# Routing tokens to pages of 128 rows per expert in a four-layer block (attention, experts, RWKV, experts)

## The chip, the cores and the metric

The kernel runs on one core of one Trainium2 chip. The metric is the device time of one execution in microseconds (us); all data are float32 in device memory before and after.

## The reference

`x` has 8 sequences of 512 tokens and 128 channels. It passes four layers, each `x = x + layer(layernorm(x))`: causal attention, a mixture of experts, an RWKV block (with layernorms of its own), and the same mixture of experts again. Cut to the experts, which the change is about:

```python
scores = softmax(xf @ Wg)                       # xf: 4096 tokens x 128, 32 experts
weights, indices = top_k(scores, 4)
C = 4 * (4096 * 4) // 32                        # 2048: tokens that one expert takes at most
for e in range(32):
    pos = nonzero(pair_expert == e, size=C)     # the first C (token, expert) pairs in token order
    xg = xf[tok]
    out = (silu(xg @ W1[e]) * (xg @ W3[e])) @ W2[e] * w[:, None]     # 64 hidden units
    y = y.at[tok].add(out)
z = (silu(xf @ Ws1) * (xf @ Ws3)) @ Ws2         # the shared expert, 128 hidden units
return y + z
```

The RWKV block runs a recurrence over the tokens, which the kernel does with scans along the free axis on VectorE, and a channel mix with a hidden width of 512 whose hidden values are `relu(.)**2`.

## The kernel before

A sequence is held as four tiles of 128 tokens (`NJ`). Each layer is a generator that issues a few instructions per step.

- `attention(b)` (from L277): layernorm, four transposes (`turn`, L153), Q, K, V, then four blocks of scores, softmax, transposes and products, and then `route(x, 0, b)`.
- `rwkv(b)` (from L351): two layernorms one behind the other (`norm`, L137, each with an addition and a power on POOL, L146 and L147), projections, three scans, four reciprocals, the output projection, the channel mix, then `route(x, 1, b)`. Ten of its elementwise operations on 128x512 are on POOL, and the four squares of L449.
- `route(xa, f, b)` (L160): layernorm, the scores `lg`, the four largest (`chosen`, L194), running counts per expert (L201 on POOL, L205 and L206 on PE), and gates: the score where an expert was chosen and has room, else zero. The gates are transposed and stored to `gd` in memory (L216).
- `experts(f, b)` (L230): all 32 experts on all 512 tokens. Two experts fill 128 partitions, so 16 pairs, plus the shared expert as step 0. A pair has two matmuls into PSUM, `a` (L251) and `c` (L253), tanh on ACT (L257), a DVE operation (L258), a multiplication by the gates on DVE (L263), a product on POOL (L264), and a matmul that accumulates into `y` (L239). Where the gate is zero, the work is done and contributes nothing. The gates of four pairs are read back from `gd`, each over 64 partitions, by two loads on SP's queue (L224): eight loads per call.

The sequences go through the layers one behind the other: in step `s` of the loop at L477, `experts(0, s-1)` is interleaved with `attention(s)`, and `experts(1, s-3)` with `rwkv(s-2)`, one step of the experts to two of the other. A scheduler then orders the instructions of each engine by dependences and priorities, so the order is near the written one and not equal to it. Engines work in order and wait for one another by semaphores.

Of the kernel before, what the change touches and what calls it, by code (L numbers as in the profile page):

```python
# [9 lines left out]
F32 = mybir.dt.float32  # L10
AF = mybir.ActivationFunctionType
ALU = mybir.AluOpType
AX = mybir.AxisListType
PSUM = bass.MemoryType.PSUM

P = 128          # partitions, tokens of a tile, channels
B = 8            # sequences
S = 512          # tokens of a sequence
NJ = S // P      # token tiles of a sequence
E = 32           # experts  # L20
NP = E // 2      # expert pairs: two experts of 64 hidden units fill 128 partitions
NQ = NP // 4     # gate loads of a sequence, each for four pairs
TOPK = 4
CAP = 4 * (B * S * TOPK) // E   # tokens that one expert takes at most
# [3 lines left out]
# Columns of the packed [128, .] weights.  # L28
# [9 lines left out]
# Columns of the packed per-channel vectors.  # L38
# [4 lines left out]
def interleave(heavy, light):  # L43
    """Traces two streams of work side by side: two steps of the light one behind each of the heavy one."""
    for _ in heavy:
        for _ in range(2):
            next(light, None)
    for _ in light:
        pass
# [3 lines left out]
def kernel(ctx: ExitStack, tc: tile.TileContext, x, small, vecs, w13, w2, out):  # L53
# [3 lines left out]
    xin = ctx.enter_context(tc.tile_pool(name="xin", bufs=3))  # L57
    wk2 = ctx.enter_context(tc.tile_pool(name="wk2", bufs=2))
    wk1 = ctx.enter_context(tc.tile_pool(name="wk1", bufs=1))
    mo = ctx.enter_context(tc.tile_pool(name="mo", bufs=3))  # L60
    gates = ctx.enter_context(tc.tile_pool(name="gates", bufs=2))
    st = ctx.enter_context(tc.tile_pool(name="st", bufs=3))
    dram = ctx.enter_context(tc.tile_pool(name="dram", bufs=2, space=bass.MemoryType.DRAM))
    ps_m = ctx.enter_context(tc.tile_pool(name="ps_m", bufs=2, space=PSUM))
    ps_y = ctx.enter_context(tc.tile_pool(name="ps_y", bufs=1, space=PSUM))
    ps_l = ctx.enter_context(tc.tile_pool(name="ps_l", bufs=3, space=PSUM))

# [15 lines left out]
    w13s = const.tile([P, NP, 2, P], F32, tag="w13", name="w13s")  # L83
    w2s = const.tile([P, NP, P], F32, tag="w2", name="w2s")
    for q in range(NQ):
        nc.sync.dma_start(out=w13s[:, 4 * q : 4 * q + 4], in_=w13[:, 4 * q : 4 * q + 4])
        nc.sync.dma_start(out=w2s[:, 4 * q : 4 * q + 4], in_=w2[:, 4 * q : 4 * q + 4])
    load_x(1)

# [15 lines left out]
    tri = const.tile([P, P], F32, tag="tri", name="tri")     # tri[i, t] = i <= t  # L105
# [3 lines left out]
    nhalf = const.tile([P, NJ], F32, tag="nhalf", name="nhalf")  # L109
    nc.gpsimd.memset(nhalf, -0.5)  # L110
    wdec = const.tile([P, 1], F32, tag="wdec", name="wdec")  # -exp(time_decay)
    nc.scalar.activation(wdec, V("time_decay"), AF.Exp)
    nc.vector.tensor_scalar(wdec, wdec, -1.0, None, ALU.mult)

    # Scores and the values looked for in them, each behind or before four marks that every row
    # has: the match below then finds just the four largest, the first of equals first.
    sc, lst, tot = [], [], []
    for f in range(2):
        s = const.tile([P, NJ, E + 4], F32, tag=f"sc{f}", name=f"sc{f}")
        m = const.tile([P, NJ, 8], F32, tag=f"lst{f}", name=f"lst{f}")  # L120
        for i in range(4):
            nc.gpsimd.memset(s[:, :, E + i : E + i + 1], -1.0 - i)
            nc.gpsimd.memset(m[:, :, 4 + i : 5 + i], -1.0 - i)
        t = wk2.tile([P, NJ + 1, E], F32, tag=f"tot{f}", name=f"tot{f}_start")
        nc.gpsimd.memset(t[:, NJ, :], 0.0)
        sc.append(s)
        lst.append(m)
        tot.append(t)
# [8 lines left out]
    def norm(src, dst, name):  # L137
        """dst = (src - mean) / sqrt(var + eps) over the channels of [128 tokens, 4, 128]."""
        stats = st.tile([P, NJ, 6], F32, tag="stats", name=f"stats_{name}")
        mv = st.tile([P, NJ, 2], F32, tag="mv", name=f"mv_{name}")  # L140
        rstd = st.tile([P, NJ], F32, tag="rstd", name=f"rstd_{name}")
        for j in range(NJ):
            nc.vector.bn_stats(out=stats[:, j, :], in_=src[:, j, :])
        for j in range(NJ):
            nc.vector.bn_aggr(out=mv[:, j, :], in_=stats[:, j, :])  # L145
        nc.gpsimd.tensor_scalar(rstd, mv[:, :, 1], EPS, None, ALU.add)  # L146
        nc.gpsimd.tensor_tensor(rstd, rstd, nhalf, ALU.pow)  # L147
# [5 lines left out]
    def turn(src, name):  # L153
        """[128 tokens, 4, 128 channels] -> PSUM [128 channels, 512 tokens], or back."""
        p = light(f"turn_{name}")
        for j in range(NJ):
            nc.tensor.transpose(p[:, j * P : (j + 1) * P], src[:, j * P : (j + 1) * P], ident)  # L157
        return p

    def route(xa, f, b):  # L160
        """Layernorm, scores, the top four experts, capacity; gates go out over the partitions of
        their experts. Gates carry the factor 1/2 of silu(a) = a (1 + tanh(a/2)) / 2."""
        n = f"{f}_{b}"
        xn = wk1.tile([P, NJ, P], F32, tag=f"xn{f}", name=f"xn_{n}")
# [3 lines left out]
        xT = wk2.tile([P, S], F32, tag=f"fT{f}", name=f"fT_{n}")  # L168
# [7 lines left out]
        ex = wk1.tile([P, NJ, E], F32, tag=f"ex{f}", name=f"ex_{n}")  # L176
# [13 lines left out]
        rep = wk1.tile([P, NJ, E + 4], F32, tag=f"rep{f}", name=f"rep_{n}")  # L190
        for j in range(NJ):
            nc.vector.match_replace(out=rep[:, j, :], in_to_replace=m[:, j, :], in_values=s[:, j, :], imm_value=-9.0)
        chosen = wk1.tile([P, NJ, E], F32, tag=f"chosen{f}", name=f"chosen_{n}")
        nc.vector.tensor_scalar(chosen, rep[:, :, :E], -5.0, None, ALU.is_lt)  # L194
        gate = wk1.tile([P, NJ, E], F32, tag=f"gate{f}", name=f"gate_{n}")
        nc.vector.scalar_tensor_tensor(gate, s[:, :, :E], 0.5, chosen, ALU.mult, ALU.mult)
        # tot[j] counts, per place in a tile, the tokens of earlier tiles that chose an expert.
        t = wk2.tile([P, NJ + 1, E], F32, tag=f"tot{f}", name=f"tot_{n}")
        nc.gpsimd.tensor_copy(t[:, 0, :], tot[f][:, NJ, :])
        for j in range(NJ):  # L200
            nc.gpsimd.tensor_tensor(t[:, j + 1, :], t[:, j, :], chosen[:, j, :], ALU.add)  # L201
        tot[f] = t
        yield
        cum = light(f"cum_{n}")[:, : NJ * E]
        nc.tensor.matmul(cum, tri, flat(chosen), start=True, stop=False)  # L205
        nc.tensor.matmul(cum, ones, flat(t[:, :NJ, :]), start=False, stop=True)  # L206
        wt = wk1.tile([P, NJ * E], F32, tag=f"wt{f}", name=f"wt_{n}")
        nc.vector.scalar_tensor_tensor(wt, cum, float(CAP), flat(gate), ALU.is_le, ALU.mult)
        yield
        p = light(f"wT_{n}")  # L210
        for j in range(NJ):
            nc.tensor.transpose(p[:E, j * P : (j + 1) * P], wt[:, j * E : (j + 1) * E], ident)
        wT = wk1.tile([E, S], F32, tag=f"wT{f}", name=f"wT_{n}")
        nc.scalar.copy(wT, p[:E, :])
        gd = dram.tile([E, S], F32, tag=f"gd{f}", name=f"gd_{n}")
        nc.sync.dma_start(out=gd, in_=wT)  # L216
        yield
        gv = gd.rearrange("(q i two) t -> two q i t", two=2, q=NQ)

        def load_gates(q):  # L220
            """The gates of four pairs, each over the 64 partitions of its expert."""
# [307 lines left out]
```

## Time and profile before

| | |
|---|---|
| time, median of 3 runs | 1131.81 us (1131.66 to 1132.06) |
| profiled execution | 1130.8 us span |
| PE (TensorE matmul) busy | 988.6 us, 87%, 2800 instructions |
| DVE (VectorE) busy | 746.7 us, 66%, 1809 instructions |
| POOL (GpSimd) busy | 565.0 us, 50%, 613 instructions |
| ACT (ScalarE) busy | 311.6 us, 28%, 578 instructions |
| DMA | 77.38 MB, 68 GB/s mean over the span |

The profile comes from one execution, recorded by the hardware. PEld is TensorE's weight load, which overlaps PE. A line of a group has the program line, the engine, the operation, output and inputs with their shapes, the count, then busy us and the mean in ns of one, and last the idle time of the engine just before the group with what ended most of it. PEclk is the clock that TensorE was granted, 1 being full speed. A float32 matmul runs as two passes and counts as two.

### The profile page before, as it was taken

The page shows a single profiled execution, that of the slowest core. Times are in us where ns is not written, and L with a number is a line of the kernel's source. Part 1 is how long each engine was busy: PE and PEld are TensorE (multiplying, and loading weights), DVE is VectorE, ACT ScalarE, POOL GpSimd, SP SyncE. Part 2 cuts the span into 40 slices and gives each one's busy share as a digit, 9 for nine tenths or more (in the row PEclk, how much of TensorE's full clock was granted, in tenths as well). Part 3 has the DMA queues.
Part 4 walks back from the last instruction along what each step waited for, and adds up shares of the span by engine and source line. Part 5 has one row for each costly group of instructions (what it writes and reads, how often), then busy time and mean ns, then how long its engine had stood idle before and what let it go on. Part 6 is the DMA issues. An engine that isn't in the chain of part 4 may idle for free.

```text
span 1130.8 us, 9602 instructions
## 1 busy us (share of the span) xinstructions
PE 988.6 (87%) x2800; PEld 457.6 (40%) x2800; DVE 746.7 (66%) x1809; ACT 311.6 (28%) x578; POOL 565.0 (50%) x613
## 2 busy tenths in 40 slices
PE   4798988799789987998889988899889998888988
PEld 2443543344334433454334543344334443333433
DVE  2456577766866767667776678567685649588543
ACT  2231323223323332232322323232222223231221
POOL 1134345643663457534674347544484547548433
PEclk8799999999999999999999999999999999999999
DMA  5053325105332241133313240331402340142051
GB/s 184 13 118 73 81 50 112 37 13 111 78 73 50 65 96 38 45 79 80 71 38 98 59 101 17 75 86 38 114 26 50 86 112 0 38 96 65 1 123 46
DMA packets 45668, 77.38 MB, mean 68 GB/s; under 512 B 2864, under 2 KB 11184, under 8 KB 45488
## 3 DMA queue, kind: packets, MB, share of 16 engines
q1 hardware_dynamic: 45472, 76.77, 29.1%
q8 instruction: 22, 0.36, 0.1%
q14 instruction: 30, 0.25, 0.1%
q10 hardware_dynamic: 144, 0.01, 0.0%
HBM read 73.62 MB, written 3.15 MB: 68 GB/s over the span
## 4 chain that ended last, share of the span: by engine, by line
PE 47%; DVE 30%; POOL 15%; issue 4%; DMA 2%; ACT 2%; SPq 0%; POOLq 0%; DVEq 0%; ACTq 0%
PE y L239 11%; PE a L251 10%; PE c L253 10%; DVE v L263 5%; POOL h L264 4%; DVE h L258 4%; PE kk L446 3%; PE kv L459 2%; DVE wden L416 2%; PE o L325 2%; PE s L307 2%; DVE xn L149 1%; POOL rstd_f L147 1%; POOL tot L201 1%; DVE sc L184 1%
## 5 line engine op out<-in xcount | busy, mean ns | idle before, releaser
L264 POOL TENSOR_TENSOR h<-h,v 128x512 f32<-128x512 f32 x256 | 336.7, 1316 | 374.4 <-DVE v L263 299.8
L257 ACT ACTIVATE h<-a 128x512 f32<-128x512 f32 x272 | 161.5, 596 | 497.2 <-PE a L251 462.1
L251 PE MATMUL a<-fT,w13s 128*128 128x512 f32 x512 | 270.5, 612 | 11.7 <-DVE h L258 11.4
L239 PE MATMUL y<-h,w2s 128*128 128x512 f32 x512 | 265.0, 604 | 17.5 <-POOL h L264 17.5
L253 PE MATMUL c<-fT,w13s 128*128 128x512 f32 x512 | 269.3, 608 | 5.1 <-DVE v L263 5.1
L258 DVE SCALAR_TENSOR_TENSOR h<-h,a 128x512 f32<-128x512 f32 x272 | 184.7, 679 | 130.5 <-ACT h L257 129.6
L263 DVE TENSOR_TENSOR v<-c,g 128x512 f32<-128x512 f32 x256 | 174.2, 682 | 28.8 <-PE c L253 26.5
L239 PEld LDWEIGHTS y<-h,w2s 128*128 128x128 f32 x512 | 94.7, 195 | 132.0 <-issue 87.4
L253 PEld LDWEIGHTS c<-fT,w13s 128*128 128x128 f32 x512 | 96.7, 196 | 114.0 <-issue 86.9
L251 PEld LDWEIGHTS a<-fT,w13s 128*128 128x128 f32 x512 | 93.4, 196 | 107.6 <-issue 72.3
L146 POOL TENSOR_SCALAR rstd_f<-mv_f 128x4 f32<-128x4 f32 x16 | 3.6, 228 | 78.4 <-DVE mv_f L145 78.4
L149 DVE TENSOR_SCALAR xn<-x,mv_f,rstd_f 128x128 f32<-128x128 f32 x64 | 23.5, 429 | 25.5 <-POOL rstd_f L147 25.5
L446 PE MATMUL kk<-mix_ffn_tmk_c,sm 128*128 128x512 f32 x64 | 29.5, 601 | 4.8 <-DVE mix_ffn_tmk_c L345 4.8
L157 PE MATMUL turn_f<-ident,xn 128*128 128x128 f32 x64 | 16.7, 330 | 18.9 <-DVE xn L149 18.9
L325 PEld LDWEIGHTS o<-vs,prTs 128*128 128x128 f32 x160 | 23.4, 209 | 20.1 <-ACT prTs L320 18.9
L328 DVE SCALAR_TENSOR_TENSOR x<-o,aden,x 128x128 f32<-128x128 f32 x32 | 11.2, 350 | 28.5 <-PE o L325 28.4
L325 PE MATMUL o<-vs,prTs 128*128 128x128 f32 x160 | 27.4, 307 | 2.7 <-ACT prTs L320 2.7
L461 DVE SCALAR_TENSOR_TENSOR num_c<-thr_c,kv 128x512 f32<-128x512 f32 x8 | 5.5, 687 | 34.8 <-PE kv L459 34.8
L416 DVE RECIPROCAL wden<-wden 128x128 f32<-128x128 f32 x32 | 27.9, 913 | 0.0
L314 ACT ACTIVATE pr<-s,abig 128x128 f32<-128x128 f32 (+3 forms) x32 | 16.8, 524 | 36.3 <-DVE abig L311 26.9
L201 POOL TENSOR_TENSOR tot<-tot,chosen 128x32 f32<-128x32 f32 x64 | 16.9, 265 | 16.5 <-DVE chosen L194 13.3
L307 PE MATMUL s<-WKT,WQT 128*128 128x128 f32 (+3 forms) x64 | 25.0, 474 | 0.0
(173 smaller groups left out, 1169.1 us busy)
## 6 DMA issues: line engine op xcount, KB each, us to landing
g<-gd SPq DMA_DIRECT2D x128, 512.0 KB, 6.6
x<-in_x_dram SPq DMA_DIRECT2D x8, 256.0 KB, 4.2
w13s<-in_w_dram SPq DMA_DIRECT2D x4, 512.0 KB, 10.9
out_dram<-xo SPq DMA_DIRECT2D x8, 256.0 KB, 2.2
sm<-in_small_dram SPq DMA_DIRECT2D x1, 1040.0 KB, 7.2
w2s<-in_w_dram SPq DMA_DIRECT2D x4, 256.0 KB, 10.5
gd<-wT SPq DMA_DIRECT2D x16, 64.0 KB, 1.6
sm<-in_small_dram SPq DMA_DIRECT2D x1, 192.0 KB, 3.2
```

The source lines that it names most:

```text
L149: nc.vector.tensor_scalar(dst[:, j, :], src[:, j, :], mv[:, j, 0:1], rstd[:, j : j + 1], ALU.subtract, ALU.mult)
L239: nc.tensor.matmul(y, w, h, start=(i == 0), stop=(i == NP))
L251: nc.tensor.matmul(a, wa, xT, start=True, stop=True)
L253: nc.tensor.matmul(c, wb, xT, start=True, stop=True)
L257: nc.scalar.activation(h, a, AF.Tanh, scale=0.5)
L258: nc.vector.scalar_tensor_tensor(h, h, 1.0, a, ALU.add, ALU.mult)
L263: nc.vector.tensor_tensor(v, c, g[:, p % 4, :], ALU.mult)
L264: nc.gpsimd.tensor_tensor(h, h, v, ALU.mult)
L307: nc.tensor.matmul(s[:, :n], qT[:, i * P : n], kT[:, :n], start=True, stop=True)
L325: nc.tensor.matmul(o[:, :P], prT[:, j * P : (j + 1) * P], vs[:, j * P : (j + 1) * P], start=(j == 0), stop=(j == i))
L416: nc.vector.reciprocal(den[:, c * P : (c + 1) * P], den[:, c * P : (c + 1) * P])
L446: nc.tensor.matmul(p, W("WkeyT", c * P, (c + 1) * P), xk, start=True, stop=True)
```

## The change

The sequences are split into two groups of four (`G`, `GB`). Per group, each expert's tokens are collected in memory in pages of 128 rows: `xs[g]` and `ys[g]` have 96 pages (`NPAGE`), and a spare page takes what has no room. `clear` fills `xs` with zeros at the start. `route` computes a row for each of a token's four experts (from running counts, the pages begun so far and the rows still free in an expert's last page) and writes the normalized tokens there by 16 indirect DMAs of 128 rows, on POOL's queue. It also does the shared expert and keeps `base` = shared + input. `experts(f, g)` goes through the 96 pages in 24 units of four: it loads four pages, transposes them, multiplies each by the weights of the expert that owns the page, whose column is read from a table into a register of TensorE, and stores the results as rows of `ys`. `combine(f, b)` fetches the four rows of each token by 16 indirect DMAs on POOL's queue and adds them, times their gates, to `base`. In `rwkv`, elementwise operations go from POOL to DVE, the squares to ACT, and the two first norms take one set of moments. The streams at the end are new. Cut to its core (comments, names and shapes of temporaries left out):

```diff
+G = 2
+GB = B // G
+UNIT = 4
+NPAGE = -(-(GB * S * TOPK // P + E - 1) // UNIT) * UNIT
+DUMP = NPAGE * P
-def interleave(heavy, light):          # two steps of light behind each of heavy
+def interleave(*streams):              # (stream, steps): in turn, so many steps of each
...
+    def clear(g):
+        n = NPAGE // 2
+        for h in range(2):
+            nc.sync.dma_start(out=xs[g][h * n * P : (h + 1) * n * P]..., in_=zero.unsqueeze(1).to_broadcast([P, n // 2, 2 * P]))
+        nc.sync.dma_start(out=ys[g][DUMP:], in_=zero[:, :P])
+    w13s = const.tile([P, E, 2, H], F32, tag="w13", name="w13s")
+    w2s = const.tile([H, E, P], F32, tag="w2", name="w2s")
...
     def route(xa, f, b):
...
-        for j in range(NJ):
-            nc.gpsimd.tensor_tensor(t[:, j + 1, :], t[:, j, :], chosen[:, j, :], ALU.add)
-        cum = light(f"cum_{n}")[:, : NJ * E]
-        nc.tensor.matmul(cum, tri, flat(chosen), start=True, stop=False)
-        nc.tensor.matmul(cum, ones, flat(t[:, :NJ, :]), start=False, stop=True)
-        (gates, transposes, the store to gd, its loads)
+        nc.tensor.matmul(cum, ident, per_expert(o["seen"], NJ + 1), start=True, stop=False)
+        nc.tensor.matmul(cum[:, :NJ], tri, chosen, start=False, stop=False)
+        for j in range(NJ):
+            nc.tensor.matmul(cum[:, j + 1 :], ones, per_expert(chosen[:, j, :], NJ - j), start=False, stop=(j == NJ - 1))
+        (ten small operations: pages per expert, ends[:, bg, :] by a scan, fresh, gap)
+        (seven 128x128 operations: fits, adr; four max: a8; rows = the four addresses, as int32)
+        for j in range(NJ):
+            for k in range(TOPK):
+                nc.gpsimd.indirect_dma_start(
+                    out=xs[g][:, :],
+                    out_offset=bass.IndirectOffsetOnAxis(ap=rows[:, j, k : k + 1], axis=0),
+                    in_=xn[:, j, :], in_offset=None, bounds_check=DUMP + P - 1, oob_is_err=False)
+        (wt: gates in the order of rows, eight 128x128 operations and a sum; the shared expert; base)
-    def experts(f, b, xa, put):
+    def experts(f, g):
+        (of: each page's expert, summed from page_ends; table = its column, int32, in one partition)
+        def load(u):
+            nc.sync.dma_start(out=loaded[u], in_=xs[g][u * UNIT * P : (u + 1) * UNIT * P]...)
+        def up(u):
+            xg = loaded.pop(u)
+            load(u + 2)
+            _, at = nc.values_load_multi_w_load_instructions(
+                table[0:1, u * UNIT : (u + 1) * UNIT], engines=[PE], min_val=0, max_val=(E - 1) * P, ...)
+            for j in range(UNIT):
+                nc.tensor.transpose(p[:, j * P : (j + 1) * P], xg[:, j, :], ident)
+            nc.scalar.copy(xT, p)
+            for j in range(UNIT):
+                nc.tensor.matmul(ac[:, j]..., xT[:, j * P : (j + 1) * P], w13f[:, bass.ds(at[j], P)], start=True, stop=True)
+            nc.scalar.activation(h, ac[:, :, 0, :], AF.Tanh, scale=0.5)
+            nc.vector.scalar_tensor_tensor(h, h, 1.0, ac[:, :, 0, :], ALU.add, ALU.mult)
+            nc.vector.tensor_tensor(h, h, ac[:, :, 1, :], ALU.mult)
+        def down():
+            for j in range(UNIT):
+                nc.tensor.transpose(p[:H, j * P : (j + 1) * P], h[:, j, :], ident)
+            nc.scalar.copy(hT, p[:H, :])
+            for j in range(UNIT):
+                nc.tensor.matmul(o[:, j * P : (j + 1) * P], hT[:, j * P : (j + 1) * P], w2f[:, bass.ds(at[j], P)], start=True, stop=True)
+            nc.scalar.copy(flat(oc), o)
+            nc.sync.dma_start(out=ys[g][u * UNIT * P : (u + 1) * UNIT * P]..., in_=oc)
+        load(0); load(1)
+        for u in range(24): up(u); down() of the unit before
+    def combine(f, b, put):
+        for j in range(NJ):
+            for k in range(TOPK):
+                nc.gpsimd.indirect_dma_start(
+                    out=got[:, k, :], out_offset=None, in_=ys[g][:, :],
+                    in_offset=bass.IndirectOffsetOnAxis(ap=rows[:, j, k : k + 1], axis=0), ...)
+            for k in range(TOPK):
+                nc.vector.scalar_tensor_tensor(xo[:, j, :], got[:, k, :], wt[:, j, k : k + 1], xo[:, j, :] if k else base[:, j, :], ALU.mult, ALU.add)
+        put(xo)
...
     def rwkv(b):
+        yield from combine(0, b, lambda t: x2.__setitem__(b, t))
-        norm(xa, xp, f"p{b}")
-        norm(xp, xn, f"r{b}")
+        (moments of xa once; rstd of both norms by one power on POOL, 128x8; xn and xp from xa)
-        nc.gpsimd.tensor_tensor(d, h[:, 1:], h[:, :S], ALU.subtract)
+        nc.vector.tensor_tensor(d, h[:, 1:], h[:, :S], ALU.subtract)
         (the same for ev, den, e2 * v, num twice, xs; e1 and e2 now from one difference)
-            nc.gpsimd.tensor_tensor(t, t, t, ALU.mult)
+            nc.scalar.activation(t, t, AF.Square)
...
-    for s in range(B + 3):
-        (experts(0, s-1) beside attention(s), experts(1, s-3) beside rwkv(s-2))
+    interleave((of_group(0, attention), 1))
+    interleave((of_group(1, attention), 3), (experts(0, 0), 1))
+    interleave((of_group(0, rwkv), 4), (experts(0, 1), 1))
+    interleave((of_group(1, rwkv), 4), (experts(1, 0), 1))
+    interleave((experts(1, 1), 2), (last(0), 1))     # last(g): combine(1, b) and the store, b of group g
+    interleave((last(1), 1))
```

## The prediction

> **What bounds the kernel now.** I read the page first: busy shares, chain, costliest groups.
>
> ```profile
> span 1130.8 us, 9602 instructions
> PE 988.6 (87%) x2800; PEld 457.6 (40%) x2800; DVE 746.7 (66%) x1809; ACT 311.6 (28%) x578; POOL 565.0 (50%) x613
> ...
> PE 47%; DVE 30%; POOL 15%; issue 4%; DMA 2%; ACT 2%; SPq 0%; POOLq 0%; DVEq 0%; ACTq 0%
> ...
> L264 POOL TENSOR_TENSOR h<-h,v 128x512 f32<-128x512 f32 x256 | 336.7, 1316 | 374.4 <-DVE v L263 299.8
> ...
> L251 PE MATMUL a<-fT,w13s 128*128 128x512 f32 x512 | 270.5, 612 | 11.7 <-DVE h L258 11.4
> L239 PE MATMUL y<-h,w2s 128*128 128x512 f32 x512 | 265.0, 604 | 17.5 <-POOL h L264 17.5
> L253 PE MATMUL c<-fT,w13s 128*128 128x512 f32 x512 | 269.3, 608 | 5.1 <-DVE v L263 5.1
> L258 DVE SCALAR_TENSOR_TENSOR h<-h,a 128x512 f32<-128x512 f32 x272 | 184.7, 679 | 130.5 <-ACT h L257 129.6
> L263 DVE TENSOR_TENSOR v<-c,g 128x512 f32<-128x512 f32 x256 | 174.2, 682 | 28.8 <-PE c L253 26.5
> ```
>
> The routed experts own 270.5 + 265.0 + 269.3 = 804.8 us of PE's 988.6: 50.3 for each of the 16 layers of a sequence. On DVE L258 and L263 take 22.4 each time. The execution shown has 1130.8 us, 1.0 below the median of 1131.8.
>
> The columns after the bar are busy us, mean ns of one, and idle time before the group with its releaser. Second, the busy time by window; rows: attention alone; rwkv beside experts; attention beside experts. After the window and its length stand the busy us of each engine, the granted clock, the DMA share:
>
> ```profile
> core 0: us, PE busy (x) PEld busy (x) DVE busy (x) ACT busy (x) POOL busy (x), PEclk, DMA share, GB/s
> ...
> 28.00:48.00 20.00, 13.48 (x38) 8.28 (x39) 7.67 (x26) 2.86 (x7) 2.40 (x4) 0.59 0.05 14
> ...
> 409.00:482.40 73.40, 63.62 (x168) 27.83 (x167) 53.93 (x115) 19.89 (x34) 45.93 (x46) 0.98 0.22 49
> 482.40:543.60 61.20, 57.12 (x185) 28.51 (x184) 39.71 (x113) 18.76 (x38) 25.09 (x27) 1.00 0.38 88
> ```
>
> A sequence costs 73.4 + 61.2 = 134.6 us, PE 87 to 93% busy, at full clock. Where attention runs alone (28 to 48 us), the granted clock is 0.59 with PE only 67% busy. Third, the timeline (start, duration): first of that lone attention, from its first transposes to the cumulative counts of its routing, then of one rwkv, from its first transposes to its choice of experts:
>
> ```profile
> 7.00 0.73 PE L157 MATMUL turn_a<-ident,xna 128*128 128x128 f32 x2 [7.00 <-DVE xna L149]
> ...
> 52.32 0.30 PEld L206 LDWEIGHTS cum<-tot,ones 128*128 128x128 f32 x2 [0.63 <-POOL tot L201]
> ```
>
> ```profile
> 410.11 0.38 PE L157 MATMUL turn_r<-ident,xnr 128*128 128x128 f32 x2
> ```
>
> ```profile
> 479.74 0.21 DVE L194 TENSOR_SCALAR chosen<-rep 128x128 f32<-128x128 f32 x1
> ```
>
> Attention with routing alone needs 45.3 us (52.32 - 7.00); rwkv beside experts 69.6 (another 291.7 to 355.3: 63.5).
>
> **Removed.** Per group the pages hold 96 x 128 = 12288 rows, where 32 experts x 2048 tokens = 65536 were worked on. What goes is 50.3 us of PE, 22.4 of DVE and 21 of POOL (336.7/16) per layer and sequence; 128 gate loads and 16 gate stores.
>
> **Added to PE.** 96 pages in units of four are 24 units per layer and group, 6 per sequence. A unit has 16 passes of 128 columns (0.11 each start to start at full clock, 0.21 at half) and 8 transposes (L157 turn_y 0.28 each when isolated, 0.11 to 0.16 packed): 2.7 to 3.1 us, so 17 to 18 for 50.3. Alone, with PE at half clock, its chain counts: transposes 0.9, copy 0.59, up passes 1.9, tanh 0.37, two DVE operations 0.82, transposes back 1.05, copy 0.37, down passes 1.9: 7.9 in a row. PE's own part at half clock is 5 or a little less, and the next unit's up passes stand before this one's down passes, so two chains overlap: I take 5.2, between 3.1 (PE alone, full clock) and 7.9.
>
> **Added to POOL.** 256 scatters and 256 gathers, 64 KB each, t us apiece. None is in the trace. Bounds: 0.43 to 0.62 if it costs what an SP issue does (L224), 2.1 as the longest POOL operation (L404). The nearest row is
>
> ```profile
> L147 POOL TENSOR_TENSOR rstd_f<-rstd_f,nhalf 128x4 f32<-128x4 f32 x16 | 16.6, 1038 | 0.7
> ```
>
> a POOL operation whose time is spent by item rather than by streaming, as writing 128 addresses must be. I take 1.1: 512 of them are 563 us, as much as POOL does now. A page section of DMAs tells what a transfer does behind its issue (columns: KB, us to landing):
>
> ```profile
> g<-gd SPq DMA_DIRECT2D x128, 512.0 KB, 6.6
> ...
> gd<-wT SPq DMA_DIRECT2D x16, 64.0 KB, 1.6
> ```
>
> SP issues a g load every 0.62 us while each takes 6.6, and 64 KB land in 1.6, so there issue does not wait for landing. The built kernel keeps eight indirect DMAs in flight, so landing would hold POOL only if it took over eight times t.
>
> The Trainium skill, "DMA: Bandwidth & Descriptors", section "Anatomy of one DMA", speaks against the change: a GpSimd DMA costs about 2.0 us plus bytes/436e3, and small ones are nearly all overhead. That is 2.15 us for 64 KB, longer than the 1.6 of the row. If POOL were held for all of it, my sum would read about 1700; if for its first microsecond, 1188. No row here says which.
>
> **Added to SP.** 96 unit loads of 256 KB (4.2 us landing, as x) two units ahead, hidden beside 5 us units; 96 stores. Clearing the pages (12.6 MB, beside 77 now) runs under the first attentions, which read nothing from SP but x. At the end the four output stores stand among the unit loads on SP and wait for combines; covered by the two loaded units, I cost them at nothing, a few us otherwise.
>
> **Added register load on PE**, one per unit: between 0 and 1.6 (64 KB landing, the only fetch from memory of that size); I take 0.4, the issue rows of SP. [...]
>
> **DVE in an rwkv pass.** 53.9 - 22.4, plus eleven operations in place of ten on POOL (7.5 at 0.68 for 1.3 to 2.1 on POOL), less ww, qq and a norm (3.1), plus page arithmetic (6.5), six units (4.9), combine (16 x 0.35 = 5.6): 52.9. PE is 63.6 - 50.3 + 18, about 31, and may go cold between. So DVE and the chain bound the pass: I take 59.5 from 63.5 to 69.6, shorter by the POOL operations. Attention beside six units: turn_a to chosen took 37.8 and 44.4 beside experts (from 358.6 and 484.0 us); with the page arithmetic behind it I take 42.5.
>
> ACT loses 16 tanh (9.5) and gains six units (12.6) and four squares (2.4): 25 of 59.5, hidden by DVE; without that cover it would be 5 us a pass. Attention's DVE by the same terms is about 30 of 42.5.
>
> **The new order.** The four attentions of the first group now have nothing beside them; pages exist only when all four have scattered. In the built kernel's order PE has unit 0's transposes in the middle of attention 4; POOL has all scatters of sequences 4 to 7 ahead of the first group's gathers, and 31 gathers plus 16 scatters ahead of rwkv 4's rstd, on which DVE and PE wait.
>
> - Start 7.0, four attentions 4 x 45.5: 189.
> - Unit 0 waits for sequence 3's 16 scatters, a landing and a load (17.6 + 2.2 + 4.2), 11 of it covered: 202.
> - 4 x 42.5: 372. Last routing and 16 scatters 4.4 + 17.6: 394.
> - First 16 gathers, sums and norm 17.6 + 11.4: 423.
> - 4 rwkv x 59.5: 661.
> - 47 indirect DMAs ahead of rwkv 4, 53 with a landing: 714.
> - 4 x 59.5: 952.
> - At the end 31 gathers and sequence 7's 16 scatters, 50 after some overlap: 1002.
> - 24 units alone, 24 x 5.2 + 3: 1130.
> - 64 gathers, sums, store 70.4 + 8: 1208. Add 1.0: **1209**.
>
> Paired stages fall from 8 x 134.6 = 1077 to 646 (-431), unpaired ones grow from 54 (1130.8 - 1077) to 562 (+508). 206 indirect DMAs lie exposed (16 + 16 + 16 + 47 + 47 + 64): each 0.1 us of t is 21 us, and the change breaks even at t = 0.73.
>
> **Clock.** The row at 28 to 48 us holds 0.59 with PE busy two thirds. The Trainium skill, "TensorE: Matmul & The Clock Gate", section "Why this matters for your kernels", asks only that PE has no idle gaps above about 3 us; in this stage the longest was about 3.1 (2.88 before turn_f) and the clock stayed down, so the measurement decides. By the page the first attentions would be 40 us shorter.
>
> **Rivals.**
> - Faster: an indirect DMA holds POOL no longer than SP's issues do. At t = 0.6 the sum is 1209 - 0.5 x 206 = 1106, at 0.43 it is 1071; it decides below 0.73. For it: issue rows of 0.31 to 0.62. Against: those describe regular patterns, here 128 addresses come from a tile. 0.20.
> - POOL becomes the bound: at t = 1.5, 1291 by the sum, and each of 8 rwkv passes finds half a batch of 16 ahead of its rstd (12): about 1385; at 2.1, a whole batch (34): 1690. 0.14.
> - The register load drains PE: at 1.6, 24 x 1.2 plus half of that in the other 72: +72, 1280. For: PE's queue cannot run ahead of a value it needs. Against: the table stands ready early. 0.12.
> - Unnamed before: PE keeps full clock alone. 40 in the attentions and 24 x 1.3 in the last units: 1138, still slower; it lies in the main case.
> - Main: t between 0.8 and 1.4, 1147 to 1340 with the clock's share down to 1130: 0.54.
>
> **How the numbers follow.** 1209 is the main case at t = 1.1. The range 1090 to 1400 leaves out t below 0.52 (about 0.09) and t above about 1.5 (about 0.09). Differences under 0.2% (2.3 us) a measurement of this kernel can hardly tell from none. Faster: the first rival and a thin end of the main case, 0.22; same 0.02; slower 0.76.
>
> **What would show it.** Right: POOL rows of indirect DMAs near 1.1 us; no experts before about 190 us with PEclk near 0.6 there; PE idle holes near 200, 400, 670 and 950 us released by POOL or DMA; rwkv passes near 60; a tail of gathers of 70 us after the last unit. Wrong: POOL rows under 0.7 or over 1.5; full clock in the first attentions; units alone taking 3.5 or 7 us; rwkv passes above 65, which would mean that DVE's added operations are dearer than their rows.

## The result and the profile after

The changed kernel takes 1291.82 us (median of six runs) against 1131.74 for the kernel before, measured beside it: a ratio of 1.1418 with an interval of 1.1375 to 1.1461. It is slower, as forecast, and inside the range, but the loss is 160 us where the forecast had 77. Three later repeats gave 1.1429, 1.1458 and 1.1411. The execution shown here has 1284.83 us with a span of 1282.9; the sum of the prediction stood at 1208 for the span, so 75 us are to be explained. One kernel below (the first run with PE kept busy) was profiled in one of its slower executions, 1391.42 us where its median is 1384.06, so only the median is used.

The page of the changed kernel, whole lines from its busy times, its slices, its chain, its groups and its DMA issues:

```profile
span 1282.9 us, 13772 instructions
PE 739.1 (58%) x3672; PEld 534.7 (42%) x3672; DVE 634.2 (49%) x2322; ACT 356.4 (28%) x722; POOL 583.4 (45%) x617
...
PEclk7666676899975777696967559869695755699555
...
PE 33%; POOL 21%; issue 19%; DVE 14%; DMA 7%; ACT 5%; POOLq 1%; ACTq 0%; DVEq 0%
...
L334 POOL DMA_INDIRECT xs<-xn,rows x256 | 262.2, 1024 | 295.2 <-DVE same L350 219.8
L469 POOL DMA_INDIRECT got<-ys,rows x256 | 265.4, 1037 | 164.6 <-DMA ys<-oc 79.2
...
xs<-xn,rows POOLq DMA_INDIRECT x256, 2.3
got<-ys,rows POOLq DMA_INDIRECT x256, 2.6
```

No engine is busy for more than 58% of the span, and the chain is handed from one engine to the next. The two rows of indirect DMAs give what the trace of before could not: 1024 and 1037 ns busy. That looks like the 1.1 us forecast, but the busy time is not the price. The timeline of POOL in the same profile shows what lies between two of them; here from the first gathers, ahead of the first rwkv pass:

```profile
392.78 1.01 POOL L469 DMA_INDIRECT got<-ys,rows  x1 [0.30 <-issue]
```

The next starts at 394.10: 1.31 us later, of which 0.30 is idle put down to "issue", not counted as busy. Scatters with nothing beside them follow each other every 1.28 us (0.97 + 0.30). So t, the time of POOL for one indirect DMA in the prediction, is 1.28 to 1.31 us alone, and in a busy stretch more: 16 scatters from 576.37 to 598.50 took 1.38 each.

The windows of the changed kernel by stage (columns as in the windows of before; the stage from 190 to 391, attentions beside units, is left out):

```profile
0.00:190.00 190.00, 111.79 (x384) 68.25 (x385) 89.03 (x424) 37.30 (x89) 63.78 (x102) 0.69 0.39 118
...
391.00:425.00 34.00, 7.46 (x32) 6.32 (x32) 9.53 (x33) 3.10 (x6) 26.36 (x27) 0.55 0.34 97
425.00:690.00 265.00, 181.24 (x828) 126.48 (x828) 171.12 (x552) 92.00 (x174) 113.01 (x108) 0.78 0.22 64
690.00:752.00 62.00, 11.33 (x38) 7.40 (x38) 22.20 (x105) 1.68 (x4) 48.02 (x48) 0.53 0.17 49
752.00:1007.00 255.00, 180.75 (x860) 127.10 (x860) 169.24 (x540) 94.92 (x180) 102.96 (x101) 0.80 0.24 71
1007.00:1073.00 66.00, 11.44 (x39) 7.53 (x40) 21.13 (x94) 1.68 (x4) 50.87 (x51) 0.53 0.21 62
1073.00:1190.00 117.00, 86.79 (x576) 75.72 (x576) 30.64 (x80) 49.43 (x96) 29.75 (x30) 0.83 0.45 128
1190.00:1283.00 93.00, 0.00 (x0) 0.00 (x0) 23.02 (x64) 0.00 (x0) 64.82 (x64) 0.50 0.20 57
```

Four stretches (rows two, four, six and eight; called holes below) have POOL at work and the others mostly idle, 255 us together: waits for indirect DMAs. The marks of the forecast's order stand beside those of the trace so:

| stage | forecast | trace | difference of lengths |
|---|---|---|---|
| attentions, to the first gathers | 0 to 394 | 0 to 391 | -3 |
| first gathers and norm | to 423 | to 425.8 | +6 |
| four rwkv passes | to 661 | to 689 | +25 |
| 47 indirect DMAs | to 714 | to 750.2 | +8 |
| four rwkv passes | to 952 | to 1006.7 | +18.5 |
| 47 indirect DMAs, overlapping | to 1002 | to 1068.3 | +11.6 |
| 24 units alone | to 1130 | to 1190.8 | -5.5 |
| 64 gathers, sums, store | to 1208 | to 1282.9 | +14 |

The four holes are 40 us longer than forecast, the eight passes 44; the rest gives back 8.5. The first hole has another make-up than forecast: 25 gathers stand ahead of the first pass's root (`rstd_p`) and not 16; its input is ready at 415.42, and it starts at 423.72.

**A pass.** Passes are named by their sequence, counted from 0. The chain of waits in pass 2, start and duration:

```profile
597.53 0.97 POOL xs L334
...
598.52 0.27 POOL rstd_c L207
...
598.87 1.05 POOL rstd_c L208
...
599.95 0.36 DVE xnc L210
```

The variance that `rstd_c` needs was ready at 594.89 (DVE L200). It stands on POOL behind the 16 scatters of the sequence before, begun at 576.37, and starts only at 598.52: 3.6 us late, and with it xnc and the transposes. The same wait of 3.6 us lies in passes 1, 2, 3, 6 and 7, and one of 1.4 in pass 5: 19.6 us behind scatters.

In passes 0 and 4, the first of each group, no scatters stand ahead, but gathers do, for the passes that come after. DVE's waits in pass 0 (window 425 to 490; us in total, times, longest):

```profile
DVE xn L210 <- POOL rstd_f L208: 7.7, 1, 7.7
DVE xnc L210 <- POOL rstd_c L208: 7.1, 1, 7.1
```

and in pass 4 (752 to 812):

```profile
DVE xn L210 <- POOL rstd_f L208: 9.2, 1, 9.2
```

`rstd_f` is the root of the layernorm ahead of the routing; DVE has part of the moments for the next pass in its queue behind xn. In pass 0 `rstd_c` starts 6.4 us and `rstd_f` 6.7 us after its variance is ready, in pass 4 `rstd_f` 8.2: 21.4 us behind gathers. So small operations of the passes stand ready for 41 us in all while POOL issues indirect DMAs.

**Units alone.** The timeline of the changed kernel, all engines, after the last pass:

```profile
1100.31 0.38 ACT L425 ACTIVATE h<-ac 128x256 f32<-128x256 f32 x1 [0.50 <-PE ac L420]
...
1103.03 0.35 DVE L478 SCALAR_TENSOR_TENSOR xo<-got,wt,xo 128x128 f32<-128x128 f32 x1 [0.93 <-DMA got<-ys,rows]
1104.00 0.37 DVE L478 SCALAR_TENSOR_TENSOR xo<-got,wt,base 128x128 f32<-128x128 f32 x1 [0.62 <-DMA got<-ys,rows]
...
1104.29 0.41 DVE L426 SCALAR_TENSOR_TENSOR h<-h,ac 128x256 f32<-128x256 f32 x1
...
1106.19 1.03 PE L434 MATMUL hT<-ident,h 128*64 128x128 f32 x4 [5.92 <-DVE h L427]
```

ACT's tanh is done at 1100.69, but DVE has sums in its queue ahead of the unit's L426, each of which waits for a gather at 1.31 us apiece; PE waits 5.92 us for the result. Until those 33 gathers are through, four units end in 46 us (their output copies on ACT, L444, at 1094.42, 1099.22, 1110.12 and 1118.45). Then the copies come every 3.40 us (1123.21, 1126.62, 1130.02), with PE's clock at 1.00 from 1140 to 1180.

### The profile page after: what moved, and what is told of

It is laid out like the page before. It is cut to its first block, busy times and chain, and to the rows that moved or that the text cites. A ratio compares the mean times of both kernels' runs of the same rounds, so it can differ in the third digit from the quotient of the medians.

```text
span 1282.9 us, 13772 instructions
## 1 busy us (share of the span) xinstructions
PE 739.1 (58%) x3672; PEld 534.7 (42%) x3672; DVE 634.2 (49%) x2322; ACT 356.4 (28%) x722; POOL 583.4 (45%) x617
## 4 chain that ended last, share of the span: by engine, by line
PE 33%; POOL 21%; issue 19%; DVE 14%; DMA 7%; ACT 5%; POOLq 1%; ACTq 0%; DVEq 0%
POOL xs L334 9%; POOL got L469 9%; DMA got<-ys,rows 6%; PE o L439 6%; PE ac L420 5%; PE o L533 3%; PE hT L434 2%; PE s L515 2%; PE lg L245 1%; PE prT L526 1%; PE s L366 1%; PE xgT L415 1%; PE kk L664 1%; POOL rstd_f L208 1%; ACT hTs L436 1%
## 5 line engine op out<-in xcount | busy, mean ns | idle before, releaser
L334 POOL DMA_INDIRECT xs<-xn,rows x256 | 262.2, 1024 | 295.2 <-DVE same L350 219.8
L469 POOL DMA_INDIRECT got<-ys,rows x256 | 265.4, 1037 | 164.6 <-DMA ys<-oc 79.2
L439 PE MATMUL o<-w2s,hTs 64*128 x768 | 138.9, 318 | 14.3 <-ACT hTs L436 14.2
L420 PE MATMUL ac<-w13s,xgTs 128*128 x768 | 132.2, 319 | 10.1 <-ACT xgTs L417 9.0
L434 PE MATMUL hT<-ident,h 128*64 128x128 f32 x384 | 71.4, 314 | 114.2 <-DVE h L427 114.0
L439 PEld LDWEIGHTS o<-w2s,hTs 64*128 64x128 f32 x768 | 109.6, 211 | 52.9 <-ACT hTs L436 28.4
L420 PEld LDWEIGHTS ac<-w13s,xgTs 128*128 128x128 f32 x768 | 113.4, 221 | 33.8 <-ACT xgTs L417 17.8
L478 DVE SCALAR_TENSOR_TENSOR xo<-got,wt,xo 128x128 f32<-128x128 f32 x192 | 64.3, 349 | 118.4 <-DMA got<-ys,rows 117.6
L415 PE MATMUL xgT<-ident,xg 128*128 128x128 f32 x384 | 74.2, 317 | 83.7 <-DMA xg<-xs 83.7
L444 ACT COPY oc<-o 128x512 f32<-128x512 f32 x96 | 56.1, 584 | 106.6 <-PE o L439 106.5
L426 DVE SCALAR_TENSOR_TENSOR h<-h,ac 128x256 f32<-128x256 f32 x96 | 39.6, 413 | 80.0 <-ACT h L425 79.6
```

Of the source, the lines that this page charges most:

```text
L334: i = nc.gpsimd.indirect_dma_start(out=xs[g][:, :], out_offset=bass.IndirectOffsetOnAxis(ap=rows[:, j, k : k + 1], axis=0), in_=xn[:, j, : ...
L415: nc.tensor.transpose(p[:, j * P : (j + 1) * P], xg[:, j, :], ident)
L420: nc.tensor.matmul(ac[:, j].rearrange("p s h -> p (s h)"), xT[:, j * P : (j + 1) * P], w13f[:, bass.ds(at[j], P)], start=True, stop=True,)
L426: nc.vector.scalar_tensor_tensor(h, h, 1.0, ac[:, :, 0, :], ALU.add, ALU.mult)
L434: nc.tensor.transpose(p[:H, j * P : (j + 1) * P], h[:, j, :], ident)
L439: nc.tensor.matmul(o[:, j * P : (j + 1) * P], hT[:, j * P : (j + 1) * P], w2f[:, bass.ds(at[j], P)], start=True, stop=True,)
```

## The experiments

In the kernels called pinned, each engine's instructions keep the order of the changed kernel: edges without a wait are added between neighbours, so that an edit does not move other work. The edit shown is then the only one.

**A disturbance.** On three chips (1, 7 and 13) the kernels derived from the changed one ran with long waits between engines, most of them of ACT and DVE for PE's results, while POOL issued indirect DMAs. On chips 6 and 9 they ran without them; no run of the changed kernel itself is known to have been on one of the three, so what decides stays open. The kernel before and the dense one below were not touched by it. It shows as waits whose releaser is "remote"; the waits of the first kernel with an earlier rstd_c (us in total, times, longest):

```profile
ACT h L425 <- remote: 44.4, 6, 20.6
```

The longest, 20.6 us, lies beside gathers, others beside scatters. The three programs that were run on both kinds of chip took 82, 120 and 127 us longer there. So totals from chips 1, 7 and 13 are upper bounds only.

**The price of the indirect DMAs: half as many.** Every token goes to two pages in place of four, and its sum uses the two rows twice; the units are unchanged.

```diff
-            for k in range(TOPK):          # scatter, and the same at the gather
+            for k in range(TOPK // 2):
```

First with the order left to the scheduler, then pinned, twice.

> Only two of a token's four rows are scattered and gathered (256 indirect DMAs instead of 512); the sums use the two gathered rows twice, all else is unchanged. POOL theory: 206 exposed indirect DMAs at 1.3 us become 103 (134 us less) and the scatters ahead of rstd_c end 10 us earlier in each pass (about 6 x 8 = 48 less): about 1105 us. Rival, passes bound by DVE and PE: 134 less and no more, about 1150 us.

> As e2 (256 indirect DMAs instead of 512; the sums use two gathered rows twice), now with the instruction order of the changed kernel kept on every engine. Price theory: 103 fewer exposed indirect DMAs at 1.3 us, 134 less, and up to 25 less in the passes: 1133 to 1158. If the missing 75 us were mainly something else (clock, DVE), the gain would stay at 100 or less: above 1190.

> Half of the indirect DMAs (256), order kept, on a chip without the stalls that all variants of the first two calls showed. 103 fewer exposed at 1.28 to 1.30 are 133 less, the waits for rstd_c (3.8 x 7) go as well: 1290 - 160 = 1130. If only the exposed ones count: 1157.

Measured: 1141.9, 1117.69 and 1120.41 us, one execution each, all on disturbed chips. Even so the pinned ones lie 171 to 174 below the changed kernel, lower than was expected of either, and below the kernel before (1129.6 and 1131.6 beside them). The 256 DMAs left out hold 103 of the 206 that the prediction called exposed: 103 x 1.3 = 134 us. The rest fits the waits in the passes: in the last of these profiles `rstd_c` no longer waits for POOL (POOL waits 62.1 us, in seven waits, for the variance), and no `rstd_c` or `rstd_f` of the passes starts more than 1.2 us late. Its windows of passes 0 and 4, from one `rstd_p` to the next:

```profile
414.60:468.80 54.20, 38.84 (x188) 27.40 (x188) 41.40 (x119) 22.51 (x43) 24.16 (x25) 0.81 0.29 83
686.20:739.40 53.20, 41.27 (x192) 29.11 (x193) 38.50 (x107) 22.42 (x42) 22.39 (x21) 0.79 0.33 96
```

In the changed kernel they are 65.9 us long at a clock of 0.73 and 62.3 at 0.80: 21 us more, as much as the waits behind gathers, and in pass 4 with the same clock. So half of the indirect DMAs cost more than the whole loss of 160 us, and with the added arithmetic still in place the kernel is not slower than the one before.

**What the price depends on: 64 rows in place of 128** in each scatter, pinned (half of the rows are not written).

```diff
-    out_offset=bass.IndirectOffsetOnAxis(ap=rows[:, j, k : k + 1], axis=0), in_=xn[:, j, :],
+    out_offset=bass.IndirectOffsetOnAxis(ap=rows[:64, j, k : k + 1], axis=0), in_=xn[:64, j, :],
```

> Scatters move only 64 of their 128 rows (the other rows of the pages stay as they were); gathers are unchanged; order kept as in the changed kernel. If POOL's time for an indirect DMA is by row, a scatter takes about 0.5 us instead of 0.97 and the 0.30 between two stays; if it is a fixed price, 0.97 stays. By row, the 16 scatters exposed before unit 0, the 16 of the last attention, and those of rwkv 4 and of the end become 7.5 us shorter each: about 30 to 40 us less.

Measured: 1268.98 (one execution) against 1290.36 of the changed kernel beside it. From the groups of this kernel:

```profile
L334 POOL DMA_INDIRECT xs<-xn,rows x256 | 244.4, 955 | 295.4 <-DVE same L350 221.6 <-issue 72.5 <-DMA xs<-xn,rows 1.2
```

Half the addresses and half the bytes take 955 ns in place of 1022; undisturbed ones follow each other every 1.21 us in place of 1.28. The price is one per instruction, hardly one per row. The forecast chose 1.1 by the row "whose time is spent by item"; the size was near, the reason was not. Most of the 21 us lie in the passes: from the first to the last `rstd_p` it took 504.8 us against 522.1, where `rstd_c` starts 5 us earlier in all. Why the passes gain more than that was not tested.

**rstd_c behind the scatters: taken off POOL.** All inverse roots by a bit guess and three Newton steps on DVE, order left to the scheduler.

```diff
-    nc.gpsimd.tensor_tensor(rstd, rstd, nhalf[:, :NJ], ALU.pow)
+    rstd = rsqrt(rstd, NJ, name)     # nc.vector: 11 small operations
```

> The reciprocal roots of all norms are computed on DVE (a guess from the bits and three Newton steps, 12 small operations) and no longer by a power on POOL. POOL theory: in each rwkv pass the power for rstd_c stands on POOL behind the 16 scatters of the sequence before (16 x 1.28 = 20.4 us) and PE and DVE wait for it; a pass took 64 to 66 us where 59.5 were forecast. Without it a pass should take about 59 (8 x 6 = 48 us less), rwkv 4 should wait for its own 16 gathers and no longer for 47 indirect DMAs (40 less) and rwkv 0 for 16 instead of 25 (12 less): about 1190 us. Rival, DVE and PE are what lengthens the pass (eleven operations moved to DVE, PE at half clock): passes stay at 65 or grow by the Newton steps, only the 52 of the two waits go: about 1235 us.

Measured: 1412.56, ratio 1.2492 (1.243 to 1.2555), on chip 1. Neither expectation came true. The disturbance and a new order of all engines lie in this number; it tells nothing about the order on POOL.

**rstd_c moved ahead, pinned.** In passes 1 to 3 and 5 to 7 the two operations of rstd_c are placed ahead of the block of scatters. The scatters carry no order among themselves, so that in the built kernel only one of the 16 came behind rstd_c.

```diff
-    POOL: 16 x xs<-xn,rows; rstd_c, rstd_c
+    POOL: 15 x xs<-xn,rows; rstd_c, rstd_c; 1 x xs<-xn,rows
```

> The instruction order of the changed kernel is kept on every engine by edges without waits; on POOL alone the two operations of rstd_c of the sequences 1, 2, 3, 5, 6, 7 are moved ahead of the 16 scatters of the sequence before them. POOL theory: DVE waited 34.2 us in all for rstd_c, which started right behind the scatters; those waits go in six of eight passes: about 25 us less than the changed kernel, 1267. Rival, the chain of rwkv on DVE and PE sets the pass and the scatters hide beside it: no change, 1287 to 1297.

> q1 once more (rstd_c ahead of the scatters on POOL), beside the changed kernel on the same chip. POOL theory: 15 to 30 us less than the changed kernel of this call. Rival, chain of DVE and PE: equal within 5. If 65 us more as on the other chip while the changed kernel has 1290: then the stalls belong to the program, and the edit causes them.

Measured: 1358.2 on chip 7 (disturbed), and on chip 9 1276.58, ratio 1.1302 (1.1274 to 1.133) against 1.1458 (1.142 to 1.1496) of the changed kernel beside it: 19 us less. From the first to the last `rstd_p` it took 507.0 us against 519.5. The edit shortens the wait and does not end it: `rstd_c` is still 2.3 us late in four of the six passes and 8.9 us earlier in all. In the profiles a further 8 us lie ahead of the passes, in the attentions, whose length differs by up to 11 us between the four profiles of the changed kernel too.

**The clock alone: PE kept busy in the first attentions.** 628 transposes whose result nobody reads are placed where PE waits in the first four attentions; all else is pinned.

```diff
+    fill = ps_o.tile([P, S], F32, tag="o", name="fill")
+    for _ in range(628):
+        nc.tensor.transpose(fill[:, :P], ident, ident)   # spread over PE's waits by the order
     interleave((of_group(0, attention), 1))
```

> Order kept as in the changed kernel; in the first four attentions 628 dummy transposes into an unused PSUM tile fill the time in which PE waits for other engines (0.11 us each at full clock), all else is unchanged. Clock theory: PE then stays busy, the granted clock of the first 190 us goes from 0.69 to about 1, and the four attentions end about 35 us earlier: about 1255. Rival, the chain there is bound by DVE, ACT and handoffs: same or up to 20 us slower (dummies in the way).

> p5 once more (dummy transposes in the first four attentions), beside the changed kernel on the same chip. Clock theory: about 35 us less than the changed kernel of this call, the first attentions at a granted clock near 1. Rival, chain by DVE, ACT and handoffs: equal or up to 20 more.

Measured: 1384.06 on chip 7 (disturbed); on chip 9 1264.41, ratio 1.1179 (1.115 to 1.1208) against 1.1458: 31 us less. The same window of the changed kernel beside it and of this one:

```profile
54.00:200.00 146.00, 88.09 (x290) 55.44 (x288) 71.60 (x342) 27.52 (x68) 59.63 (x66) 0.61 0.13 45
```

```profile
54.00:200.00 146.00, 120.98 (x822) 96.69 (x820) 71.91 (x333) 33.55 (x81) 66.16 (x73) 0.91 0.20 65
```

With more work on PE the granted clock goes from 0.61 to 0.91, and the fourth sequence's scatters start at 159.0 in place of 193.4. So the low clock of attention alone costs 31 to 34 us in this pair; the prediction had put 40 on it.

**Both together.** The fillers, and rstd_c ahead of the last three scatters of the block, this time with an edge to each scatter.

```diff
-    POOL: 16 x xs<-xn,rows; rstd_c, rstd_c
+    POOL: 13 x xs<-xn,rows; rstd_c, rstd_c; 3 x xs<-xn,rows
```

> Both effects at once: the dummy transposes of p5 in the first four attentions, and rstd_c of six sequences ahead of the last three scatters on POOL (mv_c is ready 3.8 us before rstd_c starts, in each pass). If both explain what they are said to explain, they add: 31 of p5 and 6 x 3.8 = 23: 1290 - 54 = 1236, and rwkv passes of 62 instead of 65.5. If the passes are held by something else: 1260 as p5.

> c1 once more: dummy transposes in the first four attentions, and rstd_c of six sequences ahead of the last three scatters on POOL. If the two effects add: 50 us less than the changed kernel of this call (1240 where that has 1290), rwkv passes of 62 to 63 instead of 65.5. If the passes are held by something else than rstd_c's place: 31 less.

Measured: 1358.74 on chip 13 (disturbed); on chip 9 1232.21, ratio 1.0905 (1.0843 to 1.0967) against 1.1411 (1.1343 to 1.1478): 60 us less where 50 were expected if the two effects add: they do, and something more. POOL's timeline in this kernel (pass 1):

```profile
501.08 0.97 POOL L334 DMA_INDIRECT xs<-xn,rows  x1 [0.30 <-issue]
503.99 0.23 POOL L207 TENSOR_SCALAR rstd_c<-mv_c 128x4 f32<-128x4 f32 x1 [1.93 <-DVE mv_c L200]
```

Now POOL waits for the variance. First to last `rstd_p` took 497.9 us, 21 less than 519.3 in the changed kernel beside it and 27 less than the 524.5 with fillers alone. Counted to the last `rstd_f`, so that pass 7 is in, it is 555.1 against 581.9, 27 less, where the waits that went make 19. The waits behind gathers are untouched: 6.4, 6.4 and 8.1 us.

**The register load.** No load from the table; the experts' columns are fixed by the unit's number, so that tokens meet the wrong weights.

```diff
-    _, at = nc.values_load_multi_w_load_instructions(table[0:1, ...], engines=[PE], ...)
+    at = [((u * UNIT + j) % E) * P for j in range(UNIT)]
```

> Each page is multiplied by the weights of a fixed expert (the page number modulo 32); no register load and no register operations on PE, all else is unchanged. If the register load is hidden, as the 3.4 us between units alone at full clock suggests: within 10 us of the changed kernel, units alone still 3.4 to 5. Rival, the load drains PE at each unit: 1.2 us for each of the 24 units alone and half of that for 72 others, 70 us less.

> As e3 (each page by the weights of a fixed expert, no register load), now with the instruction order of the changed kernel kept. If e3 was slow by its order and not by what it left out, this runs within 10 us of the changed kernel (1282 to 1302), and shows that the register load costs nothing. Rival, the load drains PE: 70 us less. Third, the 84 us of e3 stay (1375): then neither order nor load explains them, and the granted clock is to be read.

> Weights of fixed experts, no register loads on PE, order kept. If the load is hidden: 1280 to 1300. Rival, the load drains PE at each unit: about 70 less.

Measured: 1375.79 with a free order, 1373.23 and 1366.73 pinned, one execution each, all disturbed, so the totals settle nothing. What they do show is the pace of units alone: output copies every 3.40 us (1193.90, 1197.31, 1200.71 in the last), the same 3.40 as in the changed kernel with its loads. There the register load costs nothing. Beside attention and rwkv it was not separated.

**The new rwkv alone.** The kernel before, with its dense experts, and only the new rwkv (the roots of two norms in one POOL operation, and several of rwkv's operations on DVE in place of POOL).

```diff
-    def shifted(...) ... def rwkv(...)      # before
+    def shifted(...) ... def rwkv(...)      # of the changed kernel, without combine
```

> The kernel before with nothing but the new rwkv (elementwise operations from POOL to DVE, squares on ACT, one set of moments for the first two norms); the experts stay dense. If DVE's operations cost by their rows, DVE gains 7.5 - 3.1 = 4.4 us in a pass of 73 where it is busy 54, POOL loses about 20: the chain of rwkv becomes shorter, and PE stays the bound: 0 to 3% faster (1100 to 1132 us). Rival, DVE is the hidden bound of the rwkv pass: 8 x 4 = 35 us slower.

Measured: 1117.69 against 1130.4 beside it, ratio 0.9874 (0.983 to 0.9918), with a profile of

```profile
PE 988.3 (89%) x2800; PEld 455.0 (41%) x2800; DVE 774.6 (69%) x1873; ACT 326.3 (29%) x610; POOL 420.3 (38%) x437
```

POOL does 145 us less than before (565.0), DVE 28 more, and PE's mean granted clock is 0.971. Beside the dense experts this part of the change gains 13 us, as expected (0 to 3%), and this kernel beats both.

**Repeats of the changed kernel** beside the others:

> The changed kernel itself once more, beside the kernel before. Several variants stall for 5 to 20 us at a time on ACT, DVE and PE behind semaphores, beside running scatters, in stages that their edits do not touch; the profile of the changed kernel shows no such stall. If the stalls come from the variants' programs: 1284 to 1296 us as before, without such stalls. If they come from the run (the chip, or how its DMAs share something), the same program now takes 1340 to 1390 us, and the variants are to be compared with this run.

> The changed kernel a third time, now in one call, on one chip, with two variants that stalled on another chip. If the stalls belong to the chip and not to the program: either all three of this call show stalls behind scatters (then 1340 to 1390 us here), or none does (then 1290 us here).

> The changed kernel once more, as the measure for c1_again on the same chip. If this chip is one of those on which PE's signals came late while POOL issued scatters, the changed kernel itself should now take about 1370 (the 1283 to 1295 of its other runs plus the 80 us that variants lost on such chips); on a chip without that, 1290.

Measured: 1290.36, 1295.3 and 1292.25, on chips 6, 9 and 9, without such waits.

## Why the prediction was right in sign and wrong in size

**The price t: mis-sized.** The term "I take 1.1" is 1.28 for a scatter and 1.31 for a gather alone. Its busy time alone, 1.02 to 1.04, fits the row of L147 (1038 ns) that it was taken from; the 0.30 between two of them was missing. Of the 206 exposed ones 174 lie in the four holes, where 174 x 0.2 makes 35 of the 40 us; the rest lies in the first hole, with its 25 gathers for 16, and in the third, where the overlap that the forecast took off did not come. The other 32 lie in the attentions' stage, which came out 3 us shorter than forecast all the same. The break-even point of t = 0.73 was never near.

The Trainium skill, "DMA: Bandwidth & Descriptors", section "Anatomy of one DMA", puts a GpSimd DMA at about 2.0 us plus bytes/436e3, by estimate 2.15 us for 64 KB. The trace's time to landing is 2.3 and 2.6, near that estimate; POOL is held for 0.97 of it, near the reading "its first microsecond", and for the 0.30 behind it.

**"4 rwkv x 59.5": the step that failed.** The passes took 62 to 68 us, 44 more in all, and in them lie 41 us in which small operations wait for POOL, a wait that the sum put at nothing.

- 19.6 us are `rstd_c` behind scatters. The order that ends this wait made the passes 27 us shorter; the order that only shortens it gained too. The prediction named this mechanism, in the rival where POOL becomes the bound, and let it begin at t = 1.5. The threshold can be read from the trace: a block starts 18.5 us ahead of the variance (576.37 and 594.89). At 1.1, 16 scatters last 17.6 and are just hidden; at the 1.38 that they take there, 22.1, they are not. So the same mis-sized t came back a second time through a cover that had 1 us of slack, where the sum used t only for the 206 that it called exposed.
- 21.4 us are `rstd_c` and `rstd_f` behind gathers in passes 0 and 4. The prediction looked for small operations behind gathers only at rwkv 4's first root. No kernel has these moved ahead; with half of the indirect DMAs they are on time, and the two passes 21 us shorter.

The main case should have priced both. Its reason in the text was wrong in any case: "DVE and the chain bound the pass" rested on 52.9 us of DVE, and DVE was busy for 171.12 of 265, 43 a pass. So its sign of being wrong, passes above 65, did appear, but not because DVE's operations are dearer than their rows.

Lengths less waits, an estimate, leave passes 0 and 4 at 53 and 54 and the other six at 61 to 65, so that little is left of the 44 in sum. What holds the six above 59.5 was not tested. PE runs at 0.78 to 0.80 of its clock in these windows; that this lengthens them is not shown.

**Units alone: right sum, wrong parts.** 24 x 5.2 + 3 = 128 came near 122.5 by luck. Twenty units took 3.40 each at full clock, the prediction's own mark of "wrong", since it had PE at half clock there; four others took 46 us as DVE stood in sums that wait for gathers, an order that the prediction did not look into. Here "full clock alone" came true and its 24 x 1.3 was eaten by another wait.

**Right.** The first four attentions (186 of 189), the clock there, attention beside units, the places and order of the four holes, their releaser, and the tail of 64 gathers. The clock's rule: the Trainium skill, "TensorE: Matmul & The Clock Gate", section "Why this matters for your kernels", asks for 4 us of unbroken work to reach full clock, which the prediction left out, and for no gaps above about 3 us to keep it. The prediction let the row at 0.59 decide, and attention alone ran at 0.61 to 0.69. Filling the gaps brought the clock back (0.91, 31 us), as the section would have it. Its 3 us are not what the trace of before shows: the clock there was 1.00 from 31.34 to 34.75 us, with PE busy for 0.73 of these 3.41 and no gap above 2.2, and 0.50 from 34.75 to 48.40.

**The rivals.** The faster one fell with t. The register load fell where units run alone. POOL as the bound came true in a smaller form: five passes wait 3.6 us, which is three scatters, one 1.4, and pass 0, with 13.1, and pass 4, with 8.2, for gathers.

**Does it add up?** The stages differ from the forecast by 40 us in the holes, 44 in the passes and -8.5 elsewhere, which is the whole 75. The two repairs are worth 31 for the clock and 19 for the waits behind scatters, 50 together; the kernel with both gained 60 (1232.21 against 1292.25). In the profiles the gain is 30 ahead of the first pass, 27 in the passes and 1 behind, so the passes gained some 8 more than their waits. Open are why, what holds six passes above 59.5, and what decides the long waits on chips 1, 7 and 13.

## What to carry to other kernels

Price a queued operation by the distance from start to start, not by its busy time: idle time between equal instructions is part of it, and with hundreds of them exposed it decides. When work is hidden behind a block of n such operations, write down the slack of that cover too, and what n times the price's upper end does to it. A small operation that everybody waits for belongs ahead of a long block on its in-order engine, and sums that wait for transfers should not stand in a queue ahead of work that does not.

## What the runs showed of the hardware that was not expected

- An indirect DMA costs POOL nearly the same for 64 rows as for 128: 0.90 against 0.97 us busy, and 0.30 between two in both.
- PE with more instructions was faster: 628 transposes added, 31 us saved, at a granted clock of 0.91 in place of 0.61.
- On chips 1, 7 and 13, not on 6 and 9, ACT and DVE waited up to 20.6 us at a time, put down to "remote", beside blocks of indirect DMAs, and the same programs took 82 to 127 us longer; what decides it was not found.
